# Router logits taken from the sum ahead of the norm, and the norm's POOL work moved one pair later

## The chip, the core and the metric

The kernel runs on one core of a Trainium2 chip. The time is device time from start to end of the program, in microseconds; before the change it is 5140.64 us (median of 3 runs, 5140.46 to 5146.97).

The engines are named as in the profile: PE multiplies matrices, PEld is its loading of the stationary operand, DVE is the vector engine, ACT the scalar engine, POOL the general engine, SP the engine whose queue issues most DMAs. Each engine takes its instructions in the order of its own queue and waits on semaphores for the others. Matmul results land in PSUM, and DVE or ACT bring them to SBUF.

## What is computed

Two layers follow each other on 8 x 1024 tokens of width 256: an attention of each token over its own 16 heads, with a norm, and then a block of attention over the first axis, a norm with gain and bias, a router that picks one of 8 experts for each token up to a capacity, the expert's two matrices, and two more norms. The part that this study is about is the middle of the second layer:

```python
y1 = _ln(x + _mha(x, in_proj_w, in_proj_b, out_proj_w, out_proj_b), ln1_g, ln1_b)

def _ln(x, g, b, eps=1e-05):
    mu = jnp.mean(x, -1, keepdims=True)
    v = jnp.mean((x - mu) ** 2, -1, keepdims=True)
    return (x - mu) * jax.lax.rsqrt(v + eps) * g + b

# _mha ends in  o @ ow.T + ob ;  _moe begins with
gates = jax.nn.softmax(xf @ wg, axis=-1)      # xf is y1, wg is 256 x 8
idx = jnp.argmax(gates, axis=-1)
```

With r = x + o @ ow.T + ob, y1 is (r - mean) * rs * g + b. So y1 @ wg equals rs * (r @ W) + b @ wg, where W is g * wg with the mean of each of its columns taken off. And r @ W is x @ W + ob @ W + o @ (ow.T @ W).

## The kernel before

`fused_kernel` runs three phases one behind the other. `phase_a` is the first layer; it writes its rows to `x1_d` in DRAM. `phase_b` is the attention of the second layer, the first norm and the router; it writes to `rows_d`, for each token, 513 numbers: y1, x + ln2_b, and the router's gate. `phase_c` turns the router's choices into a list of tokens for each expert, gathers rows, multiplies by the experts, norms and scatters.

`phase_b` works in 8 groups j of 1024 tokens (8 rows l of 128 tokens). Its loop goes from j = -1 to j = 8. A turn j does the attention of group j, the projections of group j + 1 (`nxt`) and the output, norm and router of group j - 1 (`prv`), woven together by hand. So j = -1 only fills (projections of group 0), and j = 8 only drains (output, norm and router of group 7). A turn has four parts n, one for each half of the channels c and of the blocks ib. A part runs, in this order:

- `scores` (PE, then DVE for the maxima `mx`), one piece of other work, the first half of `weights` (exponentials on ACT);
- `turn_s`: PE transposes of the part before, and their ACT copy `sT`; two pieces of other work;
- the second half of `weights`, `normed` (DVE), `weighted` (PE with `sT`; ACT copies to `oT`);
- all the rest of the part's list of other work.

The lists are written in `fills(j)` by `put(part, condition, function, arguments)`. In part 0, `output` is held until `weighted` has been issued, since it needs the whole of `oT`.

The pieces that matter here, before the change:

- `turn_x(j, l0)` (line 600): PE transposes of two rows of x, four tiles, and two DVE copies to `xT`. `project_qk` and `project_v` multiply `xT` by weights.
- `residual(j, l0)` (line 730): POOL adds x + out_b for two rows. It is called at the head of `output`.
- `output(j, l0)` (line 737): PE multiplies `oT` by `wout` for two rows into one PSUM buffer; DVE adds to `r`, and `norm_scalars` (line 66) takes statistics on DVE and, on POOL, variance + eps (line 73) and its power -1/2 (line 75), for each row.
- `normal(j, l0)` (line 753): DVE subtracts and scales (line 759), POOL multiplies by ln1_g and adds ln1_b (line 762, two operations) and makes x + ln2_b (line 763); SP writes `yx` to `rows_d` (line 766).
- `turn_y(j, l0)` (line 768): four PE transposes of y and an ACT copy `yT`. `logits` (line 781) multiplies `yT` by `wg` and DVE copies to `lg`.
- `exps` (line 802) and `choice` (line 809): softmax over the experts, the gate, a DMA of the gate to `rows_d` (line 818), and the choice, `red` and `hot`, for phase C.
- `expert_bias` (line 858): two DVE operations on a loaded piece of `w2`; `load_expert` issues that load at the head of each part on SP's queue. `expert` multiplies two experts' matrices together in turn j = 7.

PSUM buffers of these pieces are the three buffers named `fill`. `xb`, `r`, `yx` and `yT` have two buffers each, `x` has three; `load_x(j + 2)` is issued on SP's queue behind part 2 of turn j. At the head of `phase_c` SP's queue loads three experts' matrices (line 1003) into memory that phase B used, and `some(FC)` puts the first expert's 8 products on PE ahead of those that make the list of tokens.

## Time and profile before

| | us |
|---|---|
| median of 3 runs | 5140.64 |
| the profiled execution, its own time | 5189.02 |
| its span, first to last instruction | 5187.3 |
| mean granted TensorE clock | 0.974 |
| first phase, to the end of its last output matmul | 4334.5 |
| first transposes of x in phase B (turn j = -1) | 4353.1 |
| scores of group 0 (turn j = 0) | 4380.2 |
| scores of groups 1 to 7 start at | 4425.3, 4483.2, 4541.4, 4599.1, 4657.2, 4715.2, 4773.1 |
| last transposes of the attention's weights (turn j = 8) | 4836.2 |
| last instruction of the router, `hot` | 4883.3 |
| weight loads of phase C, first issue | 4888.9 |
| first gather of rows by the list of tokens | 4920.7 |

The profiled execution is about 0.9% longer than the plain runs; durations below come from it. Each line of the profile has the source line, the engine, the operation, and the tiles as output <- inputs. In time order a line gives start, length, and in brackets how long the engine was idle before it and what it waited for. A matmul of 32-bit floats shows as two instructions. The ends of PE's instructions are modelled, so the time that a run of them takes is read from start to start: in an undisturbed stretch, the four transposes of a pair take 0.47 us, the eight instructions of an output 1.7 us, the eight of a pair's logits 0.9 us, `project_qk` and `project_v` 1.7 us each.

### The profile page before, as it was taken

What the parts mean: (1) busy time and instruction counts of PE and PEld (TensorE: products, weight loads), DVE (VectorE), ACT (ScalarE), POOL (GpSimd) and SP (SyncE); (2) the same over time, 40 slices, a digit from 0 to 9 for tenths busy, and PEclk for the clock granted to TensorE, in tenths of its full rate; (3) what the DMA queues carried; (4) which work ended last, traced back from release to release, by engine and by line L of the source; (5) the groups of instructions that cost most, each with busy time, mean ns of one, the idle gap of its engine ahead of it and who ended that gap; (6) DMA issues with size and microseconds to landing.
All of it is one profiled execution on the core that took longest, in us unless ns stands there. A gap on an engine that the chain in (4) does not pass through costs nothing. (4 is left out here: it accounts for less than half of the span.)

```text
span 5187.3 us, 189704 instructions
## 1 busy us (share of the span) xinstructions
PE 4912.9 (95%) x79688; PEld 3314.9 (64%) x79688; DVE 3070.8 (59%) x6088; ACT 3360.4 (65%) x4123; POOL 3376.7 (65%) x7014
## 2 busy tenths in 40 slices
PE   7999999999999999999999999999999997888664
PEld 4666666666666666666666666666666664666552
DVE  5666565656666566666665656566656552565556
ACT  5777777777777777777777777777777773444233
POOL 5767767676677676776676667767676762444345
PEclk9999999999999999999999999999999998999786
DMA  2222222222222222222222222222222212222442
GB/s 76 47 48 49 48 48 49 48 48 46 48 49 49 46 48 48 49 46 48 48 49 47 48 48 49 46 48 49 48 48 47 48 47 63 63 68 59 127 131 88
DMA packets 575501, 286.30 MB, mean 55 GB/s; under 512 B 395057, under 2 KB 526257, under 8 KB 574641
## 3 DMA queue, kind: packets, MB, share of 16 engines
q1 hardware_dynamic: 366162, 111.51, 10.8%
q0 software_dynamic: 204800, 159.82, 10.3%
q8 instruction: 623, 10.21, 0.8%
q10 hardware_dynamic: 3680, 2.83, 0.2%
q14 instruction: 236, 1.93, 0.1%
HBM read 72.31 MB, written 33.59 MB: 20 GB/s over the span
## 5 line engine op out<-in xcount | busy, mean ns | idle before, releaser
L359 ACT ACTIVATE e<-pair 128x1024 f32<-128x1024 f32 x3072 | 2977.4, 1021 | 1236.0 <-PE pair L343 1236.0
L403 POOL DMA_DIRECT2D nd<-S x4096 | 1953.8, 485 | 608.5 <-DVE S L393 416.3
L343 PE MATMUL pair<-R,L 32*128 32x128 f32 (+1 forms) x32768 | 1606.8, 323 | 3.4 <-POOL event L314 3.4
L393 DVE COPY S<-sum 128x512 f32<-128x512 f32 x1024 | 707.2, 691 | 1469.3 <-PE sum L382 1154.2
L343 PEld LDWEIGHTS pair<-R,L 32*128 32x128 f32 x32768 | 1272.0, 186 | 50.0 <-POOL event L314 4.6
L373 PE MATMUL sum<-e,V 128*32 128x256 f32 x16384 | 1285.3, 385 | 4.9 <-DVE S L393 4.9
L300 POOL DMA_DIRECT2D R<-qm x2048 | 974.3, 483 | 74.2 <-issue 40.3
L382 PE MATMUL sum<-e,V 128*32 128x128 f32 x16384 | 823.5, 273 | 0.0
L382 PEld LDWEIGHTS sum<-e,V 128*32 128x32 f32 x16384 | 533.0, 110 | 352.5 <-issue 1.4
L373 PEld LDWEIGHTS sum<-e,V 128*32 128x32 f32 x16384 | 406.4, 109 | 236.7 <-DVE vT L241 41.8
L331 PE MATMUL pair<-late,sel 32*128 32x256 bf16 (+1 forms) x6144 | 499.3, 313 | 9.6 <-ACT e L359 9.6
L254 DVE COPY V<-vT 32x128 f32<-32x128 f32 x2048 | 457.9, 224 | 28.1
L412 DVE RECIPROCAL att<-nd 128x256 f32<-128x256 f32 x256 | 447.4, 1748 | 8.0 <-DMA nd<-S 4.1
L331 PEld LDWEIGHTS <-sel 32*128 32x128 bf16 x6144 | 155.4, 91 | 460.4 <-issue 445.0
L314 POOL MEMSET event<- 1x1 f32 x256 | 22.8, 89 | 615.0 <-DMA R<-qm 398.6
L234 PEld LDWEIGHTS ps<-xT,wv 128*128 128x128 f32 x2048 | 238.2, 191 | 44.4 <-issue 41.8
L223 PE MATMUL ps<-wk,xT 128*128 128x512 f32 x512 | 255.7, 622 | 11.1 <-DMA wk<-in_Wk 10.3
L234 PE MATMUL ps<-xT,wv 128*128 128x128 f32 x2048 | 262.6, 281 | 1.6 <-DVE vT L241 0.8
L266 PE MATMUL ps<-wq,xT 128*128 128x512 f32 x512 | 255.5, 622 | 6.1 <-DVE k L224 6.1
L443 PE MATMUL ps<-wo,attT 128*128 128x256 f32 x1024 | 257.8, 395 | 0.7 <-ACT attT L426 0.7
L443 PEld LDWEIGHTS ps<-wo,attT 128*128 128x128 f32 x1024 | 186.0, 191 | 63.7 <-issue 41.8
L73 POOL TENSOR_SCALAR ve<-mv 128x1 f32<-128x1 f32 x128 | 37.0, 289 | 271.2 <-DVE mv L71 269.7
(191 smaller groups left out, 3867.0 us busy)
## 6 DMA issues: line engine op xcount, KB each, us to landing
R<-qm POOLq DMA_DIRECT2D x2048, 32.0 KB
nd<-S POOLq DMA_DIRECT2D x4096, 16.0 KB
L<-k SPq DMA_DIRECT2D x4088, 8.0 KB
rows_d<-yx SPq DMA_DIRECT2D x32, 512.0 KB
xT<-in_xT SPq DMA_DIRECT2D x64, 128.0 KB
xr<-in_x SPq DMA_DIRECT2D x64, 128.0 KB
x_d<-x1o SPq DMA_DIRECT2D x64, 128.0 KB
x<-x_d SPq DMA_DIRECT2D x8, 1024.0 KB
```

What stands on the lines that cost most here:

```text
L234: nc.tensor.matmul(ps[:, i * P : (i + 1) * P], w["v"][:, c, ch * P : (ch + 1) * P], xT_of[t][:, c, :], start=c == 0, stop=c == DC - 1,)
L254: nc.vector.tensor_copy(V[32 * aa : 32 * aa + 32, qd % 2, :, qd // 2, :, aa, 0:4], src[32 * qd : 32 * qd + 32, :, ww, :, aa, :],)
L300: moved.append((None, nc.gpsimd.dma_start(R[:, b, s, b, :], q[:, b, s, cols])))
L331: nc.tensor.matmul(bank[u].rearrange("p (n i) -> p n i", i=n)[:, :, 0:32], sel[pr].rearrange("p a j -> p (a j)"), late[pr, None, :].to_bro ...
L343: one = nc.tensor.matmul(bank[u][:, x * 4 * n : (x + 1) * 4 * n].rearrange("p (b i) -> p b i", i=n), Lt[pr, 2 * (h0 + h) + jb].rearrange(" ...
L359: nc.scalar.activation(e, pair[i], AF.Exp)
L373: nc.tensor.matmul(dst[32 * u : 32 * u + 32], Vs[ww][:, 0, h0 + h, u, :], e0[u // 2][:, u % 2, x * 256 : (x + 1) * 256].rearrange("p (b i) ...
L382: nc.tensor.matmul(dst[32 * u : 32 * u + 32, :, 32:], Vs[ww][:, 1, h0 + h, u, :], e1[u // 2][:, u % 2, h * 128 : (h + 1) * 128].rearrange( ...
L393: nc.vector.tensor_copy(S[:, :, 2 * which : 2 * which + 2, :].rearrange("p b h i -> p h b i"), ps.rearrange("p (h b i) -> p h b i", h=2, b=4),
L403: nc.gpsimd.dma_start(tok[:, b, s, h0 * C1 : (h0 + G) * C1], Sx[:, 4 if s else b, b, :])
L412: nc.vector.reciprocal(att[:, cols], nd[:, 1, cols])
L443: nc.tensor.matmul(ps[:, :D], attT[:, c, :], wo[:, c, :], start=c == 0, stop=c == HID // P - 1)
```

## The change

- The logits no longer come from y. Once, in turn j = -1, `center` makes W (and W * out_b and wg * ln1_b), and `beside` makes out_w.T-times-W, which becomes 8 more columns of `wout`, and the two row sums `wrow`. `turn_x` also copies its transposes as they are, on ACT, to `xl`; `logits_x` multiplies them by W for the next group. `output` gives 264 columns: 256 for r, 8 to be added to the logits. `exps` multiplies by rs and adds the row ln1_b @ wg.
- `turn_y`, `yT` and `logits` are gone.
- `output` works on one row at a time, each in a PSUM buffer of its own.
- `residual` is a piece of its own, placed a pair ahead of its output. `normal` keeps the DVE half; the POOL half and the write are `finish`, placed behind the statistics of the next pair.
- In the drain (`last`) the `normal` and `finish` of the last pair come behind `exps` and `choice`.

The loads of `out_w` (256 KB, SP's queue) and of three columns (256 elements each, ACT's queue) are new.

```diff
-        wout = wp.tile([P, DC, D], FP, name="wout")
-        nc.sync.dma_start(wout, a["out_wT"].rearrange("(c p) f -> p c f", p=P))
+        wout = wp.tile([P, DC, D + E], FP, name="wout")
+        nc.sync.dma_start(wout[:, :, :D], a["out_wT"].rearrange("(c p) f -> p c f", p=P))
+        outw = wp.tile([P, DC, D], FP, name="outw")
+        nc.sync.dma_start(outw, a["out_w"].rearrange("(c p) f -> p c f", p=P))
+        cols = {}
+        for n in ("ln1_g", "ln1_b", "out_b"):
+            cols[n] = wp.tile([P, DC], FP, name=f"col_{n}")
+            nc.scalar.dma_start(cols[n], a[n].rearrange("(c p) -> p c", p=P), allow_slow_non_contiguous=True)
...
+        def center():
+            w = ww[:, :, 0, :]
+            nc.vector.tensor_tensor(w, wg, column("ln1_g"), ALU.mult)
+            ps = pf.tile([P, 512], FP, name="fill")
+            for c in range(DC):
+                nc.tensor.matmul(ps[:, :E], keep["ones"], w[:, c, :], start=c == 0, stop=c == DC - 1)
+            mean = wp.tile([P, E], FP, name="mean")
+            nc.vector.tensor_scalar(mean, ps[:, :E], 1.0 / D, None, ALU.mult)
+            nc.vector.tensor_tensor(w, w, mean[:, None, :].to_broadcast([P, DC, E]), ALU.subtract)
+            nc.vector.tensor_tensor(ww[:, :, 1, :], w, column("out_b"), ALU.mult)
+            nc.vector.tensor_tensor(ww[:, :, 2, :], wg, column("ln1_b"), ALU.mult)
+
+        def beside():
+            ps = pf.tile([P, 512], FP, name="fill")
+            for k in range(DC):
+                for c in range(DC):
+                    nc.tensor.matmul(
+                        ps[:, k * E : (k + 1) * E],
+                        outw[:, c, k * P : (k + 1) * P],
+                        ww[:, c, 0, :],
+                        start=c == 0,
+                        stop=c == DC - 1,
+                    )
...
+            nc.vector.tensor_copy(wout[:, :, D:], ps[:, : DC * E].rearrange("p (k e) -> p k e", k=DC))
+            nc.vector.tensor_copy(wrow, sums.rearrange("p (k e) -> p k e", k=2))
...
+            xl = kp.tile([P, 4, P], FP, name="xl")
+            nc.scalar.copy(xl, ps)
+            G["xl", j, l0] = xl
...
         def residual(j, l0):
...
-            return xb
-
-        def output(j, l0):
-            xb = residual(j, l0)
+            G["xb", j, l0] = xb
+
+        def logits_x(j, l0):
...
+                    nc.tensor.matmul(
+                        ps[:, l * E : (l + 1) * E],
+                        G["xl", j, l0][:, 2 * l + c, :],
+                        ww[:, c, 0, :],
...
+            nc.vector.tensor_tensor(
+                G["lg", j][:, l0 : l0 + 2, :],
+                ps[:, : 2 * E].rearrange("p (l e) -> p l e", l=2),
+                wrow[:, 0:1, :].to_broadcast([P, 2, E]),
+                ALU.add,
+            )
+
+        def output(j, l):
...
+            ps = pf.tile([P, 512], FP, name="fill")
+            for c in range(DC):
+                nc.tensor.matmul(
+                    ps[:, : D + E], G["oT", j][:, c, l, :], wout[:, c, :], start=c == 0, stop=c == DC - 1
+                )
+            nc.vector.tensor_tensor(r, ps[:, :D], xb, ALU.add)
+            lg = G["lg", j][:, l, :]
+            nc.vector.tensor_tensor(lg, ps[:, D : D + E], lg, ALU.add)
+            scalars.append(norm_scalars(r, G["rs", j][:, l : l + 1]))
 
         def normal(j, l0):
-            r, sc = G["r", j, l0]
+            r, _, sc = G["r", j, l0]
             yx = kp.tile([P, 2, 2 * D], FP, name="yx")
             y = yx[:, :, :D]
-            G["y", j, l0] = y
             for l in range(2):
                 nc.vector.tensor_scalar(y[:, l, :], r[:, l, :], sc[l][0], sc[l][1], ALU.subtract, ALU.mult)
+            G["yx", j, l0] = yx
+
+        def finish(j, l0):
+
+            yx = G["yx", j, l0]
+            y = yx[:, :, :D]
             both = [P, 2, D]
...
-        def turn_y(j, l0):
...
-        def logits(j, l0):
...
         def exps(j):
             lg = G["lg", j]
+            nc.vector.tensor_tensor(lg, lg, over_experts(G["rs", j]), ALU.mult)
+            nc.vector.tensor_tensor(lg, lg, wrow[:, None, 1, :].to_broadcast([P, L, E]), ALU.add)
...
+            last = j == NJ
+            put(0, j < 0, center)
+            put(0, O, residual, prv, 0)
+            put(0, O, residual, prv, 2)
             put(0, N, turn_x, nxt, 0)
             put(0, N, turn_x, nxt, 2)
+            put(0, j < 0, beside)
+            put(0, N, logits_x, nxt, 0)
+            put(0, O, output, prv, 0)
             put(0, N, turn_x, nxt, 4)
-            put(0, O, output, prv, 0)
+            put(0, N, logits_x, nxt, 2)
+            put(0, O, output, prv, 1)
             put(0, N, turn_x, nxt, 6)
+            put(0, O, normal, prv, 0)
+            put(0, O, residual, prv, 4)
+            put(0, N, logits_x, nxt, 4)
+            put(0, X, expert_bias, EARLY + j, 0)
+            put(0, N, project_qk, nxt, 0, 0, 0)
             put(0, O, output, prv, 2)
-            put(0, X, expert_bias, EARLY + j, 0)
-            put(0, O, normal, prv, 0)
-            put(0, N, project_qk, nxt, 0, 0, 0)
+            put(0, N, logits_x, nxt, 6)
+            put(1, O, output, prv, 3)
+            put(1, N, project_qk, nxt, 0, 0, 1)
+            put(1, O, finish, prv, 0)
             put(1, O, normal, prv, 2)
-            put(1, O, turn_y, prv, 0)
+            put(1, O, residual, prv, 6)
             put(1, O, output, prv, 4)
-            put(1, N, project_qk, nxt, 0, 0, 1)
-            put(1, O, logits, prv, 0)
-            put(1, O, normal, prv, 4)
-            put(1, O, turn_y, prv, 2)
             put(1, X, expert_bias, EARLY + j, 1)
             put(1, N, project_v, nxt, 0)
-            put(1, O, logits, prv, 2)
+            put(1, O, output, prv, 5)
             put(1, N, project_qk, nxt, 0, 1, 0)
-            put(2, O, turn_y, prv, 4)
+            put(1, O, finish, prv, 2)
+            put(1, O, normal, prv, 4)
             put(2, O, output, prv, 6)
             put(2, N, project_qk, nxt, 0, 1, 1)
-            put(2, O, logits, prv, 4)
-            put(2, O, normal, prv, 6)
+            put(2, O, output, prv, 7)
             put(2, X, expert_bias, EARLY + j, 2)
             put(2, N, project_v, nxt, 2)
+            put(2, O, finish, prv, 4)
+            put(2, O and not last, normal, prv, 6)
             put(2, N, project_qk, nxt, 1, 0, 0)
             put(2, N, project_v, nxt, 4)
-            put(3, O, turn_y, prv, 6)
+            put(2, O and not last, finish, prv, 6)
+            put(3, O, exps, prv)
             put(3, N, project_qk, nxt, 1, 0, 1)
             put(3, N, project_v, nxt, 6)
-            put(3, O, logits, prv, 6)
-            put(3, O, exps, prv)
             put(3, X, expert_bias, EARLY + j, 3)
+            put(3, O, choice, prv)
+            put(3, last, normal, prv, 6)
+            put(3, last, finish, prv, 6)
             put(3, N, project_qk, nxt, 1, 1, 0)
-            put(3, O, choice, prv)
             put(3, N, project_qk, nxt, 1, 1, 1)
```

## The prediction, made before the change was run

> **What bounds the kernel now.** I read the page's busy times first, then the busy time by stage, then the timeline of one turn of the second phase and of its end. The page:
>
> ```profile
> PE 4912.9 (95%) x79688; PEld 3314.9 (64%) x79688; DVE 3070.8 (59%) x6088; ACT 3360.4 (65%) x4123; POOL 3376.7 (65%) x7014
> ```
>
> PE carries the span, but the first phase (to 4334.6 us) and the third are not edited; only the second is. Its stages (start:end, length, then busy time of PE, PEld, DVE, ACT and POOL, granted clock, DMA share, GB/s) are: filling (j = -1), the first turn, a steady turn, the last turn, and the drain:
>
> ```profile
> core 0: us, PE busy (x) PEld busy (x) DVE busy (x) ACT busy (x) POOL busy (x), PEclk, DMA share, GB/s
> 4353.00:4380.16 27.16, 26.14 (x80) 16.00 (x81) 5.79 (x12) 4.82 (x7) 1.21 (x1) 0.85 0.13 42
> 4380.16:4425.25 45.09, 37.65 (x227) 23.98 (x227) 20.21 (x36) 20.98 (x78) 0.00 (x0) 0.92 0.13 41
> ...
> 4541.44:4599.05 57.61, 51.09 (x329) 36.54 (x328) 36.27 (x82) 25.29 (x85) 27.63 (x32) 0.97 0.30 74
> ...
> 4773.09:4836.20 63.11, 49.55 (x312) 40.74 (x312) 37.88 (x74) 20.97 (x79) 29.44 (x32) 0.84 0.32 84
> 4836.20:4883.40 47.20, 21.94 (x107) 18.13 (x105) 13.80 (x43) 4.78 (x8) 24.97 (x31) 0.67 0.12 45
> ```
>
> Six steady turns take about 58 us each. The drain has PE, DVE and POOL each busy half the time or less: a chain, not a load. The steady turn by its four parts:
>
> ```profile
> 4541.44:4554.90 13.46, 10.95 (x79) 8.02 (x79) 8.51 (x24) 4.98 (x19) 2.79 (x5) 1.00 0.31 22
> 4554.90:4573.98 19.08, 15.08 (x91) 10.82 (x91) 12.08 (x26) 6.85 (x22) 14.74 (x17) 0.91 0.22 70
> 4573.98:4587.39 13.41, 13.41 (x88) 10.00 (x89) 8.78 (x17) 6.93 (x22) 7.58 (x9) 1.00 0.19 60
> 4587.39:4599.05 11.66, 11.66 (x75) 7.71 (x74) 6.90 (x17) 6.52 (x22) 2.52 (x3) 1.00 0.55 157
> ```
>
> Parts 2 and 3 keep PE full; parts 0 and 1 do not. Part 1 in time order (start, length, instruction, idle before it and its releaser), then its granted clock (the third number from the end) in two windows:
>
> ```profile
> 4561.13 0.66 PE L774 MATMUL fill<-ident,yx 128*128 128x128 f32 x4 [3.92 <-POOL yx L762]
> ...
> 4564.37 1.80 PE L717 MATMUL fill<-sT,v 128*64 128x128 f32 x16
> ...
> 4567.42 0.69 DVE L750 TENSOR_TENSOR r<-fill,xb 128x512 f32<-128x512 f32 x1 [6.19 <-POOL xb L732]
> ```
>
> ```profile
> 4557.20:4561.10 3.90, 0.01 (x1) 0.00 (x0) 3.87 (x7) 1.34 (x8) 3.38 (x5) 1.00 0.00 0
> 4561.10:4566.10 5.00, 4.97 (x28) 3.83 (x28) 0.13 (x1) 2.96 (x12) 4.92 (x4) 0.66 0.51 141
> ```
>
> PE, in order, waits at turn_y for POOL's norm; then its clock is 0.66 for 5 us; and x + out_b, queued behind POOL's six norm operations, holds a PSUM buffer. The drain repeats the first wait four times (9, 4 and 6 us visible) and ends in logits, choice, gate, and only when the gate has landed do the third phase's weight loads issue:
>
> ```profile
> 4852.40 1.12 PE L774 MATMUL fill<-ident,yx 128*128 128x128 f32 x4 [8.72 <-POOL yx L762]
> ...
> 4876.52 1.12 PE L774 MATMUL fill<-ident,yx 128*128 128x128 f32 x4 [6.04 <-POOL yx L762]
> ...
> 4880.28 0.17 DVE L795 COPY lg<-fill 128x16 f32<-128x16 f32 x1 [6.55 <-PE fill L786]
> ...
> 4882.28 0.36 SPq L818 DMA_DIRECT2D rows_d<-gate  x1
> ...
> 4888.87 0.37 SPq L1003 DMA_DIRECT2D w<-in_w1T  x1
> ```
>
> **Instructions per turn.** PE loses 16 transposes of y (four start to start in 0.47 us, so 1.9 us). Its logits stay (32 instructions in 4 x 0.9 us), now from x. Output has 264 columns for 256: 32 instructions of 0.213 us grow by 3%, 0.2 us. PE: 47.4 us of work (summed from starts) becomes 45.7. DVE: four r of 0.69 (691 ns) become eight of 0.425 (the 128x256 row L448): +0.64; eight adds of 8 columns at 0.167 (L795): +1.3; logits_x adds against copies: 0; two products in exps at 0.225: +0.45. So 36.3 becomes 38.7 us. ACT swaps the yT copy for xl, both 0.59; POOL issues the same operations elsewhere. Each pair's output takes two fill buffers for one, but turn_y's is gone: 32 per turn as before, through three.
>
> **Start: +1.5 us (0 to 5).** A 256 KB load (outw) joins SP's queue ahead of wg, b1, b2's load into acc and the last x1o store; three loads of columns, 256 elements of 4 B each, join ACT's. 256 KB at the 350 GB/s seen in the drain is 0.75 us; bqk, 512 such elements issued at 4335.57, was in use at 4342.72. x arrives at 4353.0, so center (five small DVE operations, 1.2 us, and one matmul pair) finishes under that wait if the columns land by 4351; above 5 only if they come after x, since center's matmul stands ahead of turn_x on PE.
>
> **j = -1: +5 us (4 to 7).** PE is full there (26.14 of 27.16). It takes up the logits of group 0 (3.6 us warm; clock 0.85) and beside (24 short instructions, 0.7 to 1.4 us). **j = 0: +1.5 (0.5 to 4):** 3.6 us more PE, but PE idles 5.2 us there waiting for xT copies.
>
> **A steady turn, walked.** From scores at 0: mx is ready at 2.75, four exponentials (0.345 apart) to 4.26, sT to 5.3, as now. Part 0 has only turn_x(0) between transposes and weighted, not three turn_x, so PE waits from 2.65 to 5.34 (2.7 us; now 1.73). The second exponentials, behind an xl copy, end at 7.3, normed at 8.85. Then DVE has six xT copies (2.1), two outputs (1.15 each: 0.425 + 0.17 + 0.43 + 0.18 with their gaps), normal, before xT is complete at 13.85; project_qk, third output and last logits end the part at 17.4 (now 13.46): **part 0 loses 3.9**. Part 1: the first transposes need nothing of POOL; scores, output, transposes, qk, a 0.5 us wait for sT, weighted, output, v, output, qk end at 29.1: 11.7 us (now 19.08): **gains 7.4**. At its end DVE waits at normal(4) for the power of the row before, which POOL runs behind finish(0) (3.8) and x + out_b (1.27): queued behind that normal is the next mx, 2.1 us late, for which ACT and weighted wait. Part 2: 13.3 (13.4 now); part 3, with exps' DVE operations and exponential ahead of the weights: 11.1 (11.66). Sum 53.5, next mx 1 us late: 54.5 against 57.9.
>
> Two costs on top. POOL ends finish(6) at 46.2; SP's queue holds, behind it, two yx writes, the x load and w2 for part 3. x then has 10 us until its transposes (11.3 now): covered. w2 took some 7.5 us from issue to use (4647.89 to 4655.44, with 0.67 of DVE waiting): expert_bias waits 2 us, choice and the next mx stand behind it: 0 to 1.8. And the clock. Row: the present part 0 gap of 1.73 us keeps 1.00, the last turn's 3.04 us is followed by doubled matmuls (L717 1.97 for 1.09), the 3.9 us by the 0.66 above. [...] I take 1.2 for both: **55.7, so 2.2 to 2.3 us gained, six times 14** (bounds 54.5 and 58: 20 and 0; 27 if the DVE waits overlap better).
>
> [...]
>
> **Last turn: -7 (-12 to -2).** No turn_y, no logits (5.5 us of PE, partly cold). By the same walk the parts are 15.5, 14.8, 13, 14 for 16.3, 21.05, 11.04, 14.7: 57.3, 6 to 7 less; the expert loads' waits stay.
>
> **Drain.** r of row 0 at 4841.0. Then DVE and POOL alternate: powers 0.85 each, finish 3.8, x + out_b 1.27. POOL: powers 0 and 1 to +3.2, x + out_b, powers 2 and 3 to 7.0, finish(0), x + out_b to 12.1, powers 4 and 5 to 13.9, finish(2) to 17.7, powers 6 and 7 to 19.4. exps starts there, hot is done at 22.9, i.e. 4863.9 (now 4883.3): 19.4 earlier. finish(4) runs to 23.2, finish(6), behind choice, to 27.4; its 512 KB write lands about 32: 4873 to 4874. The weight loads of the third phase reuse this memory, as they now wait for the gate (4888.6): 15 us earlier. Before the token list they decided (ACT waits for their first expert until 4904.68, is_low has 2.64 us to spare), so the loads' 15 counts: **-15 (-20 to -9)**. The row gathers come 30 us after; the third phase shifts whole, 0 (-2 to +3).
>
> **Sum against the profiled execution:** 1.5 + 5 + 1.5 - 14 - 7 - 15 = -28 of 5189.0 (span 5187.3). The plain runs have a median of 5140.6; the stages edited do not explain that 0.9%, so I subtract the same 28: **5112 us**, own range 5098 to 5127.
>
> **Rivals.**
> (a) The waits only move: DVE's late mx and the clock eat the steady gain (six times 0), leaving -14: 5127 (5120 to 5140). For it: DVE at 38.7 of 55.7 us with waits in its queue; against it: part 1's 4 us plus its cold matmuls surely go. 0.22.
> (b) The bubbles close: PE's 45.7 us plus 4 us of waits, 8 us gained per turn, 48 + 14: 5079. Against it: part 0's DVE work. 0.10.
> (c) Slower: DVE's queue becomes the loop's bound, in part 0, where POOL's power holds a normal, late mx and two outputs add up: part 0 at 20.2 and part 1 still 19.1 make 64.4, 6.5 lost per turn: 39 - 14 = +25, 5166. It decides from a turn of 60.3 us on (57.9 plus 14/6). 0.10.
> (d) It nets to nothing, mainly if the start's columns come late: 5140. 0.08.
> Forecast: 0.50.
>
> A difference under 0.2% (10 us) cannot be told from none. Faster (below 5130): 0.50 + 0.13 of (a) + 0.10 + a little of (d): 0.75; same 0.14; slower 0.11. The range takes in (a) and most of (b): 5082 to 5142.
>
> **What would show it.** Turns of 54.5 to 57, no PE wait on POOL's yx, part 0 at 16 to 18 us and part 1 near 12; clock 1.00 in part 1, below it in part 0 at most; logits in j = -1, which takes 31 to 34 us; hot some 23 us after the drain's first r (41 now); first L1003 load released by the last yx write. It is wrong if turns stay at 58 or more, if x's transposes start after 4358, or if the loads of the third phase are not earlier by 9 us.

## The result, and the profile after

The changed kernel takes 5168.74 us (median of 5 runs, 5163.87 to 5173.77) beside 5145.42 us of the kernel before (5 runs): a ratio of 1.0048, 95% interval 1.0036 to 1.006. It is 23 us slower; 28 us faster was forecast. The profiled execution took 5166.8 us.

The profiled execution of the kernel before, 5189.02 us, was long in its third phase alone: 266.6 us from the first gather (4920.73) to the end. A second profile of the same kernel took 5140.61 us, with 221.5 us there and its first gather 3.3 us earlier. The changed kernel has 222.4 us there. So the whole loss is already there at the first gather: 4920.73 before, 4942.66 after.

Busy times of the page, then busy time by stage of the changed kernel. Each row has start:end, length, busy us of PE, PEld, DVE, ACT and POOL, granted clock, DMA share, GB/s. The stages are j = -1, j = 0, a steady turn (the third of six, which start at j = 1), the last turn, and the drain up to hot:

```profile
PE 4898.5 (95%) x79576; PEld 3302.7 (64%) x79576; DVE 3125.3 (61%) x6207; ACT 3357.3 (65%) x4123; POOL 3376.9 (65%) x7014
```

```profile
core 0: us, PE busy (x) PEld busy (x) DVE busy (x) ACT busy (x) POOL busy (x), PEclk, DMA share, GB/s
4353.87:4391.28 37.41, 37.35 (x124) 26.18 (x126) 7.76 (x20) 7.16 (x11) 2.52 (x2) 0.73 0.11 34
4391.28:4441.40 50.12, 44.47 (x257) 30.86 (x256) 20.90 (x40) 23.11 (x82) 0.00 (x0) 0.86 0.14 43
4564.30:4625.49 61.19, 49.47 (x313) 34.55 (x313) 42.81 (x95) 24.65 (x85) 28.69 (x32) 0.97 0.30 70
4807.15:4868.80 61.65, 45.09 (x264) 36.16 (x264) 42.75 (x87) 19.05 (x75) 29.40 (x32) 0.78 0.32 86
4868.80:4900.20 31.40, 11.49 (x58) 7.95 (x56) 18.52 (x51) 2.44 (x4) 20.26 (x27) 0.73 0.14 50
```

The steady turn has 1.6 us less PE work than before and is 3.6 us longer; VectorE is 6.5 us busier in it. Where the 22 us come from, stage by stage:

| stage | before | after | change | forecast |
|---|---|---|---|---|
| first transposes of x | 4353.12 | 4353.87 | +0.7 | +1.5 |
| j = -1, to the first scores | 27.0 | 37.4 | +10.4 | +5 |
| j = 0 | 45.1 | 50.1 | +5.0 | +1.5 |
| six turns, j = 1 to 6 | 347.8 | 365.8 | +17.9 | -14 |
| last turn | 63.1 | 61.7 | -1.5 | -7 |
| last turn_s to first gather | 84.5 | 73.9 | -10.7 | -15 |
| sum | | | +21.9 | -28 |

j = -1 varies between profiles: the second profile of before has 25.4 us for it, and five runs below in which this stage is the same as in the change (2, 5, 6, 9 and 18) have 34.1 to 34.6. Its loss is 7 to 12 us, and 10.4 in this pair of profiles.

The same steady turn by its four parts (before: 13.46, 19.08, 13.41, 11.66):

```profile
4564.30:4581.83 17.53, 13.50 (x107) 11.05 (x108) 12.36 (x36) 7.82 (x24) 2.85 (x5) 1.00 0.33 32
4581.83:4595.49 13.66, 11.64 (x71) 7.82 (x71) 9.08 (x21) 4.87 (x19) 8.67 (x10) 1.00 0.10 38
4595.49:4610.40 14.91, 12.25 (x76) 8.67 (x77) 11.39 (x22) 6.25 (x21) 10.90 (x12) 1.00 0.23 61
4610.40:4625.49 15.09, 12.08 (x63) 7.02 (x63) 9.98 (x20) 5.71 (x21) 6.26 (x5) 0.89 0.52 150
```

PE's 3.9 us wait of part 1 for Pool's norm is gone and part 1 gains 5.4 us. But parts 2 and 3, which kept PE full before, lose 1.5 and 3.4, and part 0 the 4 us that were foreseen. The longest of PE's waits in the six turns, before and then after (engine, line, what it waited for, us in total, times, longest):

```profile
PE fill L774 <- POOL yx L762: 23.2, 6, 3.9
PE fill L717 <- ACT sT L707: 11.0, 6, 2.4
```

```profile
PE fill L771 <- ACT sT L761: 50.6, 24, 3.0
PE fill L677 <- DVE lg L827: 9.9, 6, 1.7
```

One wait of 23 us on Pool has become one of 51 us on sT, now in every part. sT is copied by ScalarE behind the exponentials, these wait for mx, and mx stands in VectorE's queue. Part 3 of a turn, on VectorE, Pool and PE in time order (start, length, instruction, idle before it and its releaser):

```profile
4611.75 1.21 DVE L734 TENSOR_REDUCE mx<-sc 128x8 f32<-128x1024 f32 x1
4612.67 1.26 POOL L844 TENSOR_TENSOR yx<-yx,row_ln_b 128x512 f32<-128x512 f32 x1
4613.00 0.96 DVE L735 TENSOR_SCALAR mx<-mx 128x8 f32<-128x8 f32 x1
...
4613.89 1.32 POOL L845 TENSOR_TENSOR yx<-x,row_ln_b 128x512 f32<-128x512 f32 x1
4614.12 1.17 DVE L856 TENSOR_TENSOR lg<-lg,wrow 128x64 f32<-128x64 f32 x1
4615.17 2.49 POOL L787 TENSOR_TENSOR xb<-x,row_out_b 128x512 f32<-128x512 f32 x2
...
4615.58 0.94 DVE L859 TENSOR_TENSOR lg<-lg,top 128x64 f32<-128x64 f32 x1
...
4616.55 0.26 ACT L860 ACTIVATE lg<-lg 128x64 f32<-128x64 f32 x1 [7.09 <-DVE lg L859]
...
4619.16 1.09 PE L771 MATMUL fill<-sT,v 128*64 128x128 f32 x16 [3.01 <-ACT sT L761]
```

L735, eight columns, is 0.17 us long elsewhere and 0.96 here; L856 and L859 are 0.22 and become 1.17 and 0.94. Each ends just after the end of one of Pool's operations (L735 at 4613.96, Pool's L844 at 4613.93; L856 at 4615.29, Pool's L845 at 4615.21). ScalarE idles 7.09 us for exps' exponential, which stands ahead of the weights of the part; sT follows, PE waits 3.01 us for it, and the clock of the part falls to 0.89.

### The profile page after: what moved, and what is told of

Read it like the earlier page. It is cut to its first block, busy times and chain, and to the rows that moved or that the text cites. A ratio compares the mean times of both kernels' runs of the same rounds, so it can differ in the third digit from the quotient of the medians.

```text
span 5165.1 us, 189631 instructions
## 1 busy us (share of the span) xinstructions
PE 4898.5 (95%) x79576; PEld 3302.7 (64%) x79576; DVE 3125.3 (61%) x6207; ACT 3357.3 (65%) x4123; POOL 3376.9 (65%) x7014
## 3 DMA queue, kind: packets, MB, share of 16 engines
q0 software_dynamic: 204800, 159.82, 10.4%
## 4 chain that ended last, share of the span: by engine, by line
PE 87%; DVE 5%; ACT 3%; DMA 2%; issue 1%; POOL 1%; SPq 0%; ACTq 0%; DVEq 0%; POOLq 0%
PE pair L344 26%; PE sum L374 20%; PE sum L383 9%; PE pair L332 8%; PE ps L235 5%; PE ps L444 5%; PE ps L267 5%; PE ps L224 5%; PE ps L426 1%; PE fill L677 1%; ACT s L743 1%; DVE mx L734 1%; DVE yx L835 1%; ACT sT L761 1%; PE fill L822 0%
## 5 line engine op out<-in xcount | busy, mean ns | idle before, releaser
L224 PE MATMUL ps<-wk,xT 128*128 128x512 f32 x512 | 256.2, 623 | 10.7 <-DMA wk<-in_Wk 10.0
```

The source lines that it names most:

```text
L224: nc.tensor.matmul(ps, xT_of[t][:, c, :], w["k"][:, c, cols], start=c == 0, stop=c == DC - 1)
```

## The experiments

**Reading the experiments.** Totals stand beside the kernel before, run alongside (5141.6 to 5143.1 us, except for the last two kernels). Each profile is of one execution, so its turns go with its own time: those of 13 and 14 took 8 and 11 us more than their kernels' medians, that of 18 took 8 less, those of 6 and 10 differ by 5. Besides the total I use the turns' mean (j = 1 to 6: 57.97 before, 60.96 after) and **blocked time per turn**: for five kinds of VectorE operation, the mean in these turns less the length when nothing of Pool overlaps (normed 1.225, normal 0.40, the sign of mx 0.171, exps' and choice's products 0.225, expert_bias 0.48), times how often it runs in a turn. Before it is 2.95 us, in the change 8.75. By kind, before and in the change: normed 0 and 1.5, normal 1.0 and 2.9, the sign of mx 0.5 and 1.8, exps and choice 0 and 1.7, expert_bias 1.5 and 0.8. The rows behind that, of the change (the second number behind the bar is the mean in ns):

```profile
L754 DVE TENSOR_TENSOR s<-s,sm 128x1024 f32<-128x1024 f32 x24 | 38.5, 1603 | 0.8
L835 DVE TENSOR_SCALAR yx<-r,mv,rs 128x256 f32<-128x256 f32 x48 | 35.3, 766 | 4.6 <-POOL rs L76 4.6
L915 DVE SCALAR_TENSOR_TENSOR acc<-w,b,acc 128x256 f32<-128x256 f32 x40 | 24.1, 603 | 6.4 <-DMA w<-in_w 5.7
L735 DVE TENSOR_SCALAR mx<-mx 128x8 f32<-128x8 f32 x24 | 15.2, 632 | 0.8
L856 DVE TENSOR_TENSOR lg<-lg,wrow 128x64 f32<-128x64 f32 x6 | 7.0, 1174 | 0.2
```

and the same kinds before (exps' were at 0.225):

```profile
L700 DVE TENSOR_TENSOR s<-s,sm 128x1024 f32<-128x1024 f32 x24 | 29.4, 1225 | 0.8
L862 DVE SCALAR_TENSOR_TENSOR acc<-w,b,acc 128x256 f32<-128x256 f32 x40 | 28.2, 705 | 4.0 <-DMA w<-in_w 3.3
L759 DVE TENSOR_SCALAR yx<-r,mv,rs 128x256 f32<-128x256 f32 x48 | 23.7, 524 | 2.8 <-POOL rs L75 2.8
L681 DVE TENSOR_SCALAR mx<-mx 128x8 f32<-128x8 f32 x24 | 6.9, 287 | 0.8
```

**1. The Pool part undone** (the logits part alone).

```
 def output(j, l):
     if l % 2 == 0:
+        residual(j, l)
...
 def normal(j, l0):
...
+    finish(j, l0)
 # and the put lines of residual and finish are gone
```

> The changed kernel with the Pool part undone: x + out_b is made with the first output of its pair, and the norm of a pair ends directly behind its normal. Only the logits part of the change is left. Theory A (queues: the loss of 3.3 us per turn comes from exps standing ahead of the mx's exponentials in part 3, and from the small logits work in part 0): the powers of the next pair stand behind a norm again, turns become about 1 us longer (62 to 63), the drain 5 to 10 longer, in all +10 to +18 against the change, about 5182. Theory B (the loss is Pool's and VectorE's blocking one another, and the Pool part put the norm's operations where VectorE's short operations stand): turns fall to 58 to 59, and the whole is 5 to 15 below the change, about 5158.

5166.67 us, 2 us from the change; turns 60.64. Blocked time fell to 1.59 us, as theory B wanted, and it didn't help: a wait took its place. VectorE's waits in the six turns:

```profile
DVE r L826 <- POOL xb L787: 60.2, 18, 5.1
```

That is 10 us per turn (8.1 before: 48.6 in six); in the change the row is gone. So the Pool part did take a wait away, and paid for it with 7.2 us more of blocking. Both theories missed: with the order of the kernel before, VectorE stands still until Pool is done; with the new order it runs beside Pool and is blocked by it.

**2. exps later.**

```
-put(3, O, exps, prv)
 put(3, N, project_qk, nxt, 1, 0, 1)
 put(3, N, project_v, nxt, 6)
+put(3, O, exps, prv)
```

> The changed kernel with one line moved: exps goes from the first filler of part 3 to behind project_v(6), so that its exponential stands behind the weights on ScalarE and its VectorE operations behind the mx and behind finish(6) of Pool. Theory A: part 3 falls from 15.1 to 11.5 to 12.5 us with the clock at 1.00, a turn from 61.4 to about 58.2, six turns and the last -20, about 5148. Theory B: the short operations are only blocked in another place; part 3 falls by 1 at most, -5, about 5164. Both expect part 0 at 17.5.

5167.73 us: part 3 fell to 10.93 us, more than A wanted, and part 0 of the next turn rose to 21.99 to 24.22. Lines of one such border:

```profile
4618.80 1.00 DVE L915 SCALAR_TENSOR_TENSOR acc<-w,b,acc 128x256 f32<-128x256 f32 x2 [1.53 <-DMA w<-in_w]
...
4625.63 1.98 PE L771 MATMUL fill<-sT,v 128*64 128x128 f32 x16 [5.95 <-ACT sT L761]
```

With part 3 short, expert_bias waits for w2, choice and the next mx stand behind it, and PE waits 5.95 us for sT; L771's matmuls then take 1.98 us where 1.09 is usual. The 4 us came back with interest: the turns' mean is 62.09. The total is still as in the change, since in this profile x came 1.2 us earlier, j = -1 was 3.3 us shorter and the third phase 1.7.

**3. PE's empty slots filled.**

```
-put(0, O, residual, prv, 0)
-put(0, O, residual, prv, 2)
 put(0, N, turn_x, nxt, 0)
 put(0, N, turn_x, nxt, 2)
...
 put(0, N, logits_x, nxt, 0)
+put(0, O, residual, prv, 0)
+put(0, O, residual, prv, 2)
```

> The changed kernel with the two residuals of part 0 moved behind the first logits_x, so that turn_x(0), turn_x(2) and logits_x(0), not two Pool operations and turn_x(0), stand between the scores and weighted on PE. Theory C (part 0's loss of 4 us is PE's 2.6 us wait for sT with nothing to fill it): part 0 falls from 17.5 to about 15, turns by 2.5, about 5151. Theory A: part 0 ends with VectorE's queue (xT complete), which gains the 2 us in which VectorE waits for the first xl copy and little else: part 0 16.3 to 17, turns by 0.5 to 1.2, about 5163.

5161.56 us. Part 0 is 16.26 us in four of six turns and 16.95 to 16.99 in the others, as A said, but part 2 rose from 14.91 to 16.56, so the turn stayed at 60.86. Its profile is 5 us shorter than the change's because x landed 2.5 us earlier and the third phase took 1.7 less. Part 0's PE wait is not the loss.

**4. Pool's end of the norm left out.**

```
 def finish(j, l0):
-    for n, op in (("ln1_g", ALU.mult), ("ln1_b", ALU.add)):
-        nc.gpsimd.tensor_tensor(y, y, ...)
-    nc.gpsimd.tensor_tensor(yx[:, :, D:], ...)
+    nc.gpsimd.memset(yx[:, :, D:], 0.0)
```

> The changed kernel, leaving out the end of the norm on Pool (times ln1_g, plus ln1_b, x + ln2_b): one memset of the x half stands in its place, so y is written as normal left it. It prices Pool's work against VectorE. Theory B: the mean of mx's scaling (L735) falls to 0.17, of normed (L754) to 1.23, of the normals to 0.4, exps' four operations to 0.22; some 6 us of VectorE time go per turn, part 3 falls to 12.5, turns to 57, and with a drain some 8 shorter the whole is about 5133. Theory A: only the drain and part 2's wait for a power gain; turns at 60 to 61, about 5153.

5111.53 us, 0.9939 of the kernel before (0.9923 to 0.9956): 57 us less than the change. Its steady turn by parts:

```profile
4553.98:4571.85 17.87, 13.51 (x109) 11.06 (x109) 12.66 (x37) 7.82 (x24) 2.85 (x5) 1.00 0.34 31
4571.85:4583.68 11.83, 11.47 (x71) 7.81 (x71) 7.25 (x21) 4.87 (x19) 4.43 (x8) 1.00 0.12 44
4583.68:4596.70 13.02, 12.25 (x76) 8.66 (x77) 9.62 (x22) 6.25 (x21) 7.57 (x11) 1.00 0.32 102
4596.70:4607.93 11.23, 10.40 (x63) 6.38 (x63) 7.07 (x17) 5.71 (x21) 0.00 (x0) 1.00 0.58 163
```

The walk of the prediction had 17.4, 11.7, 13.3 and 11.1. Blocked time is 2.91 us here (2.95 before), and the turns' mean is 54.56 (the walk: 54.5). So the walk's turn is that of a kernel in which Pool blocks VectorE no more than before. In part this is luck: Pool also has half the work here (14.6 us per turn, 28.6 in the change), and the finish of 3.8 us, behind which the walk has its late mx, is one memset.

**5. The sign of mx on ScalarE.**

```
-nc.vector.tensor_scalar(mx, mx, -1.0, None, ALU.mult)
+nc.scalar.activation(mx, mx, AF.Copy, scale=-1.0)
```

> The changed kernel with one operation moved: the sign of mx (8 columns, L735) is made on ScalarE, not on VectorE, where Pool's work holds it for 0.46 us on average, 0.8 to 1.1 in parts 2 and 3. Theory B (Pool's operations block VectorE's short ones and through mx the exponentials, sT and weighted): the exponentials start 0.8 to 1.1 earlier in two parts, VectorE's 15 us of L735 go, turns fall by 1 to 1.8, about 5158. Theory Q (the loss is the order of the queues and Pool's own time, the powers and residuals that stand behind the norm; blocking is only a symptom): nothing, 5166, or 2 worse for the added hop.

5164.33 us, and turns of 60.94 in the mean: the rival's figure. The median turn, 59.65 where the change has 61.2, is what theory B forecast, and two long turns take it back. Part 2 fell to 13.77, part 3 to 13.5 in two turns, but exps was blocked for 2.44 us per turn where it had been 1.65, and two of six turns rose to 64.8 with a part 0 of 22.4 us at a clock of 0.77. Here the block taken from one operation went to the next.

**6. Pool nearly as busy, but only writing:** seven memsets in place of the three operations.

```
+    for _ in range(7):
+        nc.gpsimd.memset(yx[:, :, D:], 0.0)
```

> The changed kernel, leaving out the end of the norm as in the run before, but with seven memsets of 0.53 us each in place of its three operations, so that Pool is busy as long as in the change but only writes. Theory B: blocking is what costs; as far as a write doesn't block, normed is at 1.23, the sign of mx at 0.17, the normals under 0.6, turns at 54 to 55.5 and the drain as in the change: 5120. Theory Q: Pool's queue is as long as in the change, so turns stay at 59 to 61.5, and the whole at 5150 to 5166.

5142.03 us, between the two. Pool is busy 26.3 us per turn (28.6 in the change). Turns are at 56.7 to 58.9 but for one of 64.65 (mean 59.07, median 58.1), blocked time 4.58. What four of the five kinds took beside it:

```profile
L835 DVE TENSOR_SCALAR yx<-r,mv,rs 128x256 f32<-128x256 f32 x46 | 31.5, 714 | 4.6 <-POOL rs L76 4.6
L754 DVE TENSOR_TENSOR s<-s,sm 128x1024 f32<-128x1024 f32 x22 | 27.0, 1225 | 0.8
L911 DVE SCALAR_TENSOR_TENSOR acc<-w,b,acc 128x256 f32<-128x256 f32 x40 | 19.1, 478 | 2.6 <-DMA w<-in_w 1.9
L852 DVE TENSOR_TENSOR lg<-lg,wrow 128x64 f32<-128x64 f32 x5 | 5.9, 1181 | 0.2
```

normed and expert_bias are at their own length (1.225 and 0.478 us); the normals are held (0.714 for 0.40); exps is held too (1.181 for 0.225), by the next turn's x + out_b, which now runs beside it. Theory B priced 54 to 55.5 and missed by the normals and exps; theory Q priced 59 to 61.5. Of what the change takes more than experiment 4 per turn, 1.9 of 6.4 us by the means, or 3.1 of 7.0 by the medians, go with what Pool reads and its 2.4 us of further work; the rest, 4.5 or 3.9, stays when Pool only writes.

**7. The kernel before, without the end of the norm.** The same edit in the kernel before.

> The kernel before, leaving out the end of the norm on Pool in the same way (one memset in its place). It tells whether the kernel before pays for Pool's work as the changed one does. Theory B: in it the norm's operations stood under PE's wait of part 1, where VectorE had little to do, and cost it 2.9 us of blocking per turn and the 3.9 us wait with its cold clock; both go, turns 53 to 54.5, drain 15 to 20 shorter: about 5100. So without Pool's work the two kernels are alike within 12 us, and what the change does wrong is where it puts that work. Theory Q: the wait of part 1 alone goes, 54.5 to 55.5 per turn, about 5108; the same order as B in the total, so the turn's blocked operations decide between them.

5109.9 us: equal to experiment 4 within 2 us. Its turns are 55.2 (the change without that work 54.56). The kernel before loses 2.8 us per turn by Pool's end of the norm, the change 6.4. The difference, 3.6, is the whole loss of the six turns and more: 22 us where 17.9 were measured. Without it the change is worth nothing either way: to the first gather it loses 21.0 us up to the end of j = 0, gains 3.8 in six turns and 12.7 in the last turn and the drain.

**8. A warm PE at the start.**

```
+def warm():
+    ps = pf.tile([P, 512], FP, name="fill")
+    for k in range(30):
+        nc.tensor.matmul(ps, wi[:, 0, :P], wi[:, 0, :512], start=True, stop=True)
...
+put(0, j < 0, warm)
 put(0, j < 0, center)
```

> The changed kernel with 30 matmuls of 512 columns, whose result nobody reads, ahead of center, in the 15 us in which PE waits for the columns. Theory (j = -1 is 5 us longer than I put it because PE's clock stays at half until 4374, the logits' matmuls of 8 columns leaving it there): the clock is full when x arrives, j = -1 falls from 37.4 to about 30 us, the whole by 6 to 7, about 5160. Rival (the short matmuls are bound by their weight loads and copies, not by the clock): 35 us, the whole by 2.

5181.6 us, since thirty matmuls took 28.8 us and x's transposes moved from 4354 to 4370.6. But j = -1 itself fell to the theory's 30.8. First the change's j = -1, cut where the clock rises, then this kernel's:

```profile
4353.87:4374.00 20.13, 20.07 (x70) 15.79 (x71) 5.00 (x16) 3.25 (x6) 2.52 (x2) 0.50 0.20 63
4374.00:4391.28 17.28, 17.28 (x56) 10.40 (x56) 2.77 (x4) 3.91 (x6) 0.00 (x0) 0.99 0.00 0
```

```profile
4370.61:4401.45 30.84, 30.73 (x126) 20.93 (x127) 7.07 (x22) 7.06 (x11) 0.00 (x0) 0.89 0.00 1
```

**9. w2 loaded one part earlier, with exps late** (experiment 2 and this edit).

```
-load_expert(EARLY + j, n, False)
+for piece in (0, 1) if n == 0 else (n + 1,) if n < 3 else ():
+    load_expert(EARLY + j, piece, False)
```

> The changed kernel with exps behind project_v(6), as in the run that moved it alone, and with each w2 piece loaded one part earlier, so that the load of part 3 no longer stands on SP's queue behind the write of the pair that Pool ends last. Theory S (Pool's end of the norm reaches the loop by two ways: it holds exps' operations in part 3, and it holds SP's queue, w2 and with it expert_bias, choice and the next mx; moving exps alone only changed which is last): part 3 stays at 10.9, the wait for w2 goes, part 0 falls from 22 to 24 back to 17.5 with the clock at 1.00, turns at 57, the whole about 5142. Rival (VectorE's amount of work in part 3, not the place of the wait, makes the next mx late): part 0 stays at 21 or more, turns at 61, 5166.

5178.62 us. No wait for w2 is left in the six turns, and part 0 is 18.06 in the first of them and 19.19 to 26.26 in the others. So the rival was nearer: at the border with the 26.24 us, VectorE's own chain of normed, expert_bias, choice and mx runs from 4560.81 to 4566.20 without a wait in it, PE waits 3.68 us for sT, and the clock of that part 0 is 0.61.

**10 to 12. Repairs added one by one:** 10 is experiment 9 with 3's slots and nine warming matmuls; 11 adds the sign of mx on ScalarE; 12 was to move normal(4) and finish(2) into part 2.

> The run beside it, with two more edits: the residuals of part 0 behind the first logits_x (PE's slots filled as tried alone) and nine matmuls of 512 columns, whose result nobody reads, ahead of center, so that PE's clock is up when x arrives. Theory S: j = -1 falls from 37.4 to about 31 (30.8 was seen with a warm PE), x's transposes start by 4354, part 0 from 17.5 to 16.3, turns 55.8 to 57.5, the whole about 5130. Rival: part 2 gives the 1.2 us of part 0 back, as it did when the slots were filled alone, turns at 57 to 58, 5138.

> The run beside it, and the sign of mx on ScalarE. Theory B: part 2 and the next part lose the 0.8 to 1.1 us for which Pool holds L735; turns by 1 to 1.5 shorter than in the run beside it, about 5122. Rival (exps and normed are blocked in its place, and the sum stays): equal to the run beside it within 4 us.

> The run beside it, and normal(4) and finish(2) moved from the end of part 1 to behind project_qk and the first output of part 2, so that the mx of part 2 no longer stands on VectorE behind a normal that waits 0.77 us for its power and is held by Pool for 0.6 more. Theory A (order of the queue): part 2 falls from 13.8 to 13, turns by 0.8 to 1.5, about 5115. Theory B: finish(4) then meets other operations of VectorE, and part 3 gives it back: equal within 4 us.

5151.87 us (1.0018, 1.0009 to 1.0028), 5140.04 (0.9993, 0.9983 to 1.0003) and 5142.03 (0.9995, 0.9985 to 1.0004): 10 is 9 us slower than the kernel before, 11 and 12 cannot be told from it. In 10, j = -1 is 31.1 us and x is on time; in 11, with the same nine matmuls, it is 35.05. The sign of mx, whose 4 us alone are not clear of the noise, is worth 12 here, where exps stands elsewhere and loses 0.67 us per turn to Pool, not 2.44: PE's wait for sT in the six turns falls from 33.7 us in 10 to 20.6 in 11.

12 is the kernel of 11 a second time. Its lines changed places in the source but kept their part number 1, and each part has a list of its own, so neither list changed (part 2 is 13.77 us in both, and the traces of PE, DVE and ACT have the same instructions in the same order). Whether moving normal(4) helps stays untested; the 2 us between 11 and 12 are noise.

```
+put(2, O, output, prv, 6)
 put(1, O, finish, prv, 2)
+put(2, N, project_qk, nxt, 0, 1, 1)
 put(1, O, normal, prv, 4)
-put(2, O, output, prv, 6)
-put(2, N, project_qk, nxt, 0, 1, 1)
```

**13 to 15. sT ahead of the exponentials:** 13 in the change alone, 15 in the kernel before alone, 14 with slots, late exps, the sign of mx and nine warming matmuls (w2 as in the change).

```
     some(1)
+if before:
+    sT = turn_s(before[3])
+if live:
     weights(st, 0)
 if before:
-    sT = turn_s(before[3])
```

> The changed kernel with one order swapped: the transposes of s and their copy sT are issued ahead of the first four exponentials of a part, so that on ScalarE sT no longer waits for mx. If PE's wait for sT is the way by which a late VectorE reaches PE: weighted starts 1.3 us earlier in part 0 and, in part 2, as much earlier as mx was late; part 3 stays long, since exps' exponential is issued still earlier; turns by 1.5 to 3 shorter, 5150 to 5158. If VectorE's own amount of work bounds the parts: turns within 0.5, 5166.

> The changed kernel with five edits: sT ahead of the exponentials, exps behind project_v(6), the residuals behind the first logits_x, the sign of mx on ScalarE, nine matmuls ahead of center (w2's loads as in the change). If the waits for sT and their cold clock are what is left: part 0 at 16 to 16.5 with the clock at 1.00, the others at 13.4, 13.6 and 10.9, turns at 54.5 (the walk gave 53.5 to 55.7), about 5122. If VectorE's work bounds part 0 (choice, mx, xT, the outputs): part 0 at 18 to 19.5 as in the run without the swap, 5138.

> The kernel before with the same swap alone. In it PE waits 1.73 us for sT in part 0 and nowhere else for as long, and VectorE is seldom late: part 0 by 1 to 1.5 shorter, turns at 56.5, about 5134; if the wait only moves to the xT copies, 5142.

5163.33 us (5155.78 to 5174.18), 5155.51 (1.0025, 1.0015 to 1.0035) and 5138.77 (0.999, 0.9981 to 1.0, too near to none to call). In the profile of 13 PE's wait for sT falls from 50.6 to 19.9 us, but the turns rise to 61.9 to 66.7: the xl copy now stands behind the exponentials, PE waits for xT instead, and part 0 runs at a clock of 0.70 to 0.83. Lines of one such part 0:

```profile
4631.02 1.09 PE L771 MATMUL fill<-sT,v 128*64 128x128 f32 x16 [0.72 <-ACT sT L761]
...
4634.89 1.85 PE L799 MATMUL fill<-ww,xl 128*128 128x8 f32 x8 [2.19 <-DVE xT L666]
```

14 showed a third way by which Pool reaches the loop. In its profile, the slowest of its nine executions, part 0 is 21.7 to 28.0 us:

```profile
4612.97 1.27 POOL L850 TENSOR_TENSOR yx<-x,row_ln_b 128x512 f32<-128x512 f32 x1
...
4614.72 0.42 SPq L654 DMA_DIRECT2D x<-x_d  x1
4615.19 1.06 SPq L889 DMA_DIRECT2D w<-in_w  x1
...
4622.27 0.86 PE L664 MATMUL fill<-ident,x 128*128 128x128 f32 x4 [1.90 <-DMA x<-x_d]
4622.82 1.01 DVE L920 SCALAR_TENSOR_TENSOR acc<-w,b,acc 128x256 f32<-128x256 f32 x2 [2.33 <-DMA w<-in_w]
```

x and w2 are late: on SP's queue both stand behind the write of the pair that Pool ends last, at 4614.24.

**16. The kernel before once more.**

> The kernel before, unchanged. If its profiled execution was disturbed in the third phase alone: 5140 to 5148, first scores near 4380, turns of 58, first gather near 4921, as there, and 223 us from the first gather to the end, not 266. If the profile before was typical: 5185 to 5190.

5140.61 us, as told above.

**17 and 18. A third of the end of the norm taken from Pool, the output kept:** 17 is experiment 11 with this edit, 18 the change with it alone.

```
-nc.vector.tensor_scalar(y[:, l, :], r[:, l, :], sc[l][0], sc[l][1], ALU.subtract, ALU.mult)
+nc.vector.scalar_tensor_tensor(y[:, l, :], r[:, l, :], sc[l][0], rows["ln1_g"], ALU.subtract, ALU.mult)
...
-for n, op in (("ln1_g", ALU.mult), ("ln1_b", ALU.add)):
-    nc.gpsimd.tensor_tensor(y, y, rows[n][:, None, :].to_broadcast(both), op)
+for l in range(2):
+    nc.scalar.activation(y[:, l, :], y[:, l, :], AF.Copy, scale=G["r", j, l0][2][l][1])
+nc.gpsimd.tensor_tensor(y, y, rows["ln1_b"][:, None, :].to_broadcast(both), ALU.add)
```

> The kernel with the repairs and the sign of mx on ScalarE (5140), and the norm shared out otherwise: VectorE makes (r - mean) times ln1_g in one operation, ScalarE multiplies by the power, and Pool only adds ln1_b and makes x + ln2_b: two Pool operations of 1.27 us per pair, not three, 5.1 us less per turn. If Pool's work is the cause: part 2 and part 0 shorter by 1 to 2 in sum, turns near 55.5, the drain 3 to 5 shorter, about 5125 (below both kernels). Rival (ScalarE's queue takes the place: its two copies per pair wait for a power and stand ahead of exponentials): turns as they were or 1 longer, 5138 to 5148.

> The changed kernel with only this sharing of the norm. Without Pool's three operations the change took 5111.5, with seven writes in their place 5142. With a third of them gone, if the blocked operations fall in proportion: turns at 58.5 to 59.5, drain 3 to 5 shorter, about 5150. Rival: ScalarE's queue takes the place, 5164 or more.

Both ran on a chip on which the kernel before took 5189.69 us (16 runs), so only ratios compare. 17: 5179.39 us, **0.9982 (0.9972 to 0.9991), 10 us below the kernel before**; 18: 5205.3 us, 1.0031 (1.0019 to 1.0042) where the change has 1.0048. In 17 the turns are even, 56.5 to 58.0 (11: 55.5 to 62.1), but their mean is 57.65 (11: 57.90), not the 55.5 forecast: parts 0 and 2 lose 1.5 and 1.3 us, part 1 gets 2.5 longer. Blocked time is about 4.5 us for 5.91 (the new normal takes 0.475 us by itself), and the gain stands behind the turns: hot comes 86.4 us after the start of the last turn (11: 92.7). In 18 the last turn and the drain gain 9 us and a turn 0.5; its interval overlaps the change's, so its size stays unclear.

## Why the prediction was wrong

**The sum** was 50 us off: 32 in the six turns, 5.4 in j = -1, 3.5 in j = 0, 5.5 in the last turn, 4.3 in the drain, less 0.8 at the start.

**The step that failed** is the count of VectorE's work, 36.3 us of before and 2.4 us of new operations (38.7; measured 42.81). The 2.95 us of blocking in a turn of before was carried over with it, as if it belonged to the operations. It belonged to their meeting. Normal and expert_bias went from 2.5 to 3.7 us per turn; normed, the sign of mx and the products of exps and choice, for which the prediction added none, went from 0.5 to 5.0. Before, 14.74 of Pool's 27.63 us stood in part 1, much of it where VectorE stood still for x + out_b (0.13 us busy in the 5 us behind PE's wait, Pool 4.92); the change takes these waits out and spreads Pool's work over parts 1 to 3 (8.7, 10.9 and 6.3 us), beside normed, the sign of mx and exps. Blocked time became 8.75 us. With it at 2.91, experiment 4 has the walk's turn. That doesn't make the blocking the whole loss: experiment 4 frees Pool's queue too, and in experiment 6 the greater part of the loss (4.5 of 6.4 us by the means) stays beside a Pool that only writes, some of it by blocked normals and by exps beside x + out_b. How much of the rest is blocking and how much waiting was not separated.

Two measurements show the meeting. Operations of eight and 64 columns waited out Pool operations of 1.26 and 1.32 us (0.96 and 1.17 us above). And normed and expert_bias took 1.225 and 0.478 us in the mean beside experiment 6's Pool, 1.603 and 0.603 in the change.

**The steady turn by parts.** Part 0: 17.4 forecast, 17.5 measured (17.8 in the mean of six). Part 1: 11.7, got 13.66; a blocked normed (2.10 us) and normals. Part 2: 13.3, got 14.91; the late mx was foreseen, not the blocked L735 behind it. Part 3: 11.1, got 15.09; exps' four products were to take 0.225 us each, and the five operations took 2.6 from first to last, behind a sign of mx that took 0.96, and all of it ahead of the weights. The 1.2 us for w2 and the clock was my estimate, and no run shows the clock's share of it. In its place the gap of 2.60 us at the head of part 0 went with a part of 18.05 us in three turns of six, and of 17.53 to 17.54 in the other three. Once parts shortened, 1.2 was too small as well: experiments 2, 5 and 14 show 4 to 10 us per part 0 where mx, w2 or x came late.

**j = -1: +5, measured +10.4.** The work was right: with a clock that was up it would be 30.8 (experiment 8), +3.8. The mis-sized term was the clock: I assumed the 0.85 of before, and it stayed at 0.50 for 20 us. In runs 2, 5 and 9, with the same instructions in this stage, it was 14 to 15 us, so part of the 10.4 is chance.

**j = 0: +1.5, measured +5.0.** The upper end, 4, was exceeded; its parts 1 to 3 are much as before, and part 0 is 17.61 for 13.07, the same part-0 cost as in a steady turn, which I had not carried over.

**Last turn: -7, measured -1.5.** The forecast's own parts give 57.3 for 63.1, 5.8 less, not 7. Part 1 gained 5.2 (6.2 forecast), but part 2 went from 11.04 to 15.51 (13 forecast); without Pool's end of the norm it is 10.12.

**Drain: -15, measured -10.7.** The chain ran as walked, with hot 26 us after the first r (23 forecast, 41 before), and the loads of the third phase decide, as said. Missed were the two yx buffers, and Pool's block on exps:

```profile
4889.33 1.68 DVE L835 TENSOR_SCALAR yx<-r,mv,rs 128x256 f32<-128x256 f32 x2 [4.44 <-DMA rows_d<-yx]
...
4894.00 1.28 DVE L855 TENSOR_TENSOR lg<-lg,rs 128x64 f32<-128x64 f32 x1 [1.00 <-POOL rs L76]
...
4904.73 0.36 SPq L848 DMA_DIRECT2D rows_d<-yx  x1
4910.87 0.37 SPq L1069 DMA_DIRECT2D w<-in_w1T  x1
```

normal waits 4.44 us until the write of an earlier yx has left its buffer; about as much is missing from the 15.

**Right:** center hidden under the wait for x (+0.7), no PE wait on Pool's yx left, part 0's loss, the first loads behind the last yx write. **Rival (c)** named VectorE's queue as the bound from a turn of 60.3 us, and 5166 us; the turns came out at 60.96 and the total at 5168.74. That its total was met is luck: it had turns of 64.4, part 0 at 20.2 with part 1 still at 19.1, where parts 2 and 3 grew instead, and of the 21 us by which this was too much 18 came back in the other stages. That a late VectorE would bound the turn was right.

## What to carry to other kernels

A stall on an engine can be the place in which another engine's work does no harm: before a wait is removed, ask what ran under it and which operations it will stand beside afterwards. The excess of a mean over its minimum in the trace was here a property of the overlap, not of the operation (the sign of mx: 0.171 us alone, 0.287 in the mean before, 0.632 in the change); recount it for the new order, by listing which VectorE operations will lie beside Pool's. And small operations at the head of a chain (here eight columns ahead of every exponential) deserve that check first: here one took 0.96 us beside a Pool operation of 1.26.

## What the runs showed beyond that

- With matmuls of eight columns between the transposes and projections, PE filled j = -1 without a gap (37.35 us of 37.41), and the clock still stayed at 0.50 for 20 us; before, without them, the stage's mean was 0.85. In experiment 11 the clock was up when x arrived and fell 3.8 us later, with PE busy:

```profile
4356.03:4359.84 3.81, 3.42 (x29) 3.04 (x28) 3.48 (x10) 1.07 (x2) 2.19 (x2) 1.00 0.88 276
4359.84:4373.50 13.66, 13.56 (x44) 9.86 (x44) 2.21 (x8) 1.86 (x3) 0.00 (x0) 0.50 0.01 1
```

- The length of a gap alone didn't decide what it cost. In the change a PE gap of 2.60 us at the head of part 0 left the part's clock at 1.00 in turns 1, 3 and 5 and brought it to 0.91 in turns 2, 4 and 6 (0.50 from 4507.53 to 4510.94 in turn 2). In experiment 5 gaps of 3.13 to 3.15 in part 3 left 1.00 in two turns (parts of 13.5 us) and 0.89 in three (15.2 us), and one of 3.79 in part 0 went with 0.77; in experiment 13 two, of 0.72 and 2.19 us within 5 us, with 0.70.
- In all 32 pairs of the change VectorE's xT copies start only when ScalarE's xl copy of the same PSUM tile has ended (20.5 us of VectorE waits in six turns), though both only read; whether the order of the program or the chip does this wasn't tried.
- The third phase of the kernel before took 266.6 us in one profile and 221.5 in another, though both reached the first gather within 4 us. Experiments 17 and 18, on a chip on which all 16 runs of the kernel before took 5186 to 5194 us, had 268 and 266. So this looks like a property of the chip; the record doesn't say on which chip the first profile was taken.
